# Attention on one core: probabilities turned in 32x32 blocks on VectorE, weighted values on four row tiles of TensorE, and the attention's order taken from a list scheduler

## The chip, the cores and the metric

The kernel runs on one core of one Trainium2 chip. The metric is the device time of one execution in microseconds (us); the times given are medians of three runs. A core has five instruction streams that run side by side and wait for each other through semaphores: TensorE (matmul; PE in the profile, and PEld for its weight loads), VectorE (DVE), ScalarE (ACT), GpSimd (POOL) and SyncE (SP), which here only issues DMA transfers. Each stream runs its instructions in the order in which they stand.

## The reference

The kernel computes one gated block on four batches of 512 tokens with 256 features. Cut to what matters:

```python
xn = layernorm(x)                                     # no affine part
Q, K, V = xn @ Wq + bq, xn @ Wk + bk, xn @ Wv + bv    # 16 query heads, 4 key heads, 128 wide
scores = einsum("blhe,bmhe->bhlm", Q, K) / sqrt(128)
attn = softmax(scores + causal_mask)                  # 512 x 512 per head
ctx = einsum("bhlm,bmhe->blhe", attn, V).reshape(b, l, 2048)
r = xn + gelu(ctx @ Wo + bo)                          # exact GELU
s = (r - mean(r)) * rsqrt(var(r) + 1e-5) * gamma + beta
gate, up = split(xn @ w_gate_up.T)                    # 1024 each
g = silu((silu(gate) * up) @ w_down.T)
out = x + s * g
```

All operands are float32.

## The kernel before

Products of float32 operands are made of three matmuls each: every operand is kept as `hi` (rounded) and `lo` (the exact rest), and `product` (line 93) adds hi*hi, hi*lo and lo*hi into one bank of PSUM. In the profile these three are lines 95, 96 and 97. `split_psum` (line 82) makes the two parts out of a bank: ScalarE writes `hi` (line 86, or 89 with a bias), VectorE writes `lo` (87, or 90).

The first stage computes layer norms and the feed-forward gates of all four batches. The rest, the attention, has 64 steps `(b, g, i)`: batch, key head (with its four query heads) and tile of 128 queries. One batch and key head make a group of four steps; there are 16 groups. For each step:

- `scores` (line 416), four times, for sub-tiles of 32 queries of four heads: a product into bank `ps`, VectorE masks it and takes the row's minimum (449), ScalarE takes exp and the row's sum (460), VectorE the reciprocal (473), GpSimd scales the row (474). The scores are causal: tile `i` and sub-tile `t` see 128 i + 32 (t + 1) keys. For `i = 0` the product is one plain float32 matmul on operands `q0`, `k0` that GpSimd sums from their two parts (`whole`, line 370).
- `transposed_probs` (476), once for each of the `i + 1` blocks `j` of 128 keys: four TensorE transposes into bank `pt` (481), then `split_psum` into `pT`.
- `weighted` (486), once for each block: one product of `v` (128 keys by 128 features, stationary) and `pT` (128 keys by 512 columns: four heads, 128 queries) into bank `pc`. After the last block, `split_psum` makes `ctxT`.
- `projected` (505), once for each of the four heads: a product of 256 columns into the accumulator `py`.

A group thus has 10 blocks `j`. Besides, each group makes the queries of the next group (four products of 512 columns) and its keys, and each batch makes four tiles of values.

PSUM has eight banks: two for `ps`, two for `pt`, one each for `mm` (queries, keys, values), `c` (`pc`), `y0` and `y1` (`py`). All weights stay in SBUF, split once, when they are loaded (lines 111 and 112, on GpSimd in the attention).

The order of the attention's instructions is made in the source by sorting the pieces of a step on hand-set positions (`TUNE`, `ahead`, `chunks`), and the tile framework's own scheduler then orders the streams.

Of the kernel before, what the change touches and what calls it, by code (L numbers as in the profile page):

```python
# [17 lines left out]
P = 128  # L18
EPS = 1e-5
S = 32  # queries of a head in a tile of scores  # L20
MASK = -1e9
HIGHEST = 3.4028235e38
TUNE = {'a0': 0.119, 'a1': 0.3, 's0': 0.673, 's1': 0.335, 't0': 0.293, 't1': 0.231, 'w0': 0.519, 'w1': 0.5, 'o0': -0.076, 'o1': 0.537, 'gelu_at': (0, 1), 'gelu_pos': 0.0, 'fin_g': 1, 'fin_pos': 0.616, 'gelu_behind': 'ctx', 'qd': (1, 2, 1, 0), 'l0': 0.295, 'l1': 0.095, 'l2': 0.234, 'end': {'tab': -1.229, 'T1': 0.136, 'W1': 0.362, 'T0': 0.1, 'W0': 1.019, 'Ob': 0.072, 'Obs': 0.05, 'O1': 0.6, 'O1s': 0, 'O0': 1.0199999999999998, 'key': 'ctx', 'keyb': 'pT', 'G3': 0.1, 'F3': 0.101, 'Gb': 0.5, 'Fb': 0.65, 'vec': True}}
# [3 lines left out]
def kernel(  # L27
    ctx: ExitStack,
    tc: tile.TileContext,
    x: bass.AP,  # [B, L, D]  # L30
    wq: bass.AP,  # [D, H*E]
    bqT: bass.AP,  # [E, H]
    wk: bass.AP,  # [D, KV*E]
    bkT: bass.AP,  # [E, KV]
    wv: bass.AP,  # [D, KV*E]
    bvT: bass.AP,  # [E, KV]
    wo: bass.AP,  # [H*E, D]
    bo: bass.AP,  # [D]
    gamma: bass.AP,  # [D]
    beta: bass.AP,  # [D]  # L40
    wguT: bass.AP,  # [D, 2*INTER]
    wdT: bass.AP,  # [INTER, D]
    out: bass.AP,  # [B, L, D]
):
    """Products of float32 operands run on the tensor engine as products of two
    parts each: hi, rounded to the engine's 12 significant bits, and lo, the exact
    rest. hi*hi + hi*lo + lo*hi, summed in float32, is the float32 product."""
# [6 lines left out]
    G = H // KV  # query heads of a key head: g, g + KV, ...  # L54
    INTER = wdT.shape[0]
    NT = L // P  # token tiles of a batch
    ND = D // P  # chunks of the model dimension
    NI = INTER // P  # chunks of the inner dimension
# [7 lines left out]

    latest = {}

    @contextmanager
    def behind(*keys):  # L70
        """Queues what the block does behind these instructions on their engines."""
# [42 lines left out]
    def load_w(name, views, hi_on=None, lo_on=None):  # L114
# [12 lines left out]
        for k in range(1024 // n):  # L127
            split_sbuf(
                (w[:, 0, ts(k, n)], w[:, 1, ts(k, n)]), st[:, ts(k, n)], hi_on or nc.gpsimd, lo_on or nc.gpsimd
            )  # L130
# [618 lines left out]
```

## Time and profile before

| | us |
|---|---|
| median of 3 runs (680.44 to 681.06) | 680.44 |
| span of the profiled execution | 679.5 |
| TensorE busy | 661.7 (97%) |
| VectorE busy | 447.8 (66%) |
| ScalarE busy | 402.6 (59%) |
| GpSimd busy | 273.4 (40%) |

The profiled execution has its own time, a span of 679.5 us from its first to its last instruction; the runs shown are 0.9 us above it. A row for a group of instructions names line, engine, operation, written and read tiles, shape and count, then the busy time in us, the mean duration of one in ns, and the idle time just before them with what ended it. Durations of matmuls overlap, since matmuls are pipelined: what one costs is seen in the distance from its start to the next start, in the timeline.

### The profile page before, as it was taken

What the parts mean: (1) busy time and instruction counts of PE and PEld (TensorE: products, weight loads), DVE (VectorE), ACT (ScalarE), POOL (GpSimd) and SP (SyncE); (2) the same over time, 40 slices, a digit from 0 to 9 for tenths busy, and PEclk for the clock granted to TensorE, in tenths of its full rate; (3) what the DMA queues carried; (4) which work ended last, traced back from release to release, by engine and by line L of the source; (5) the groups of instructions that cost most, each with busy time, mean ns of one, the idle gap of its engine ahead of it and who ended that gap; (6) DMA issues with size and microseconds to landing.
All of it is one profiled execution on the core that took longest, in us unless ns stands there. A gap on an engine that the chain in (4) does not pass through costs nothing.

```text
span 679.5 us, 12006 instructions
## 1 busy us (share of the span) xinstructions
PE 661.7 (97%) x3996; PEld 581.6 (86%) x3996; DVE 447.8 (66%) x1337; ACT 402.6 (59%) x956; POOL 273.4 (40%) x490
## 2 busy tenths in 40 slices
PE   7979999999999999999999999999999999999995
PEld 6768888889889888888888898889888988888984
DVE  5864434165766766775787666668867766687867
ACT  4434333253765766677676665957666668576772
POOL 5588130720646423222353232216433323354332
PEclk8999999999999999999999999999999999999998
DMA  7753322211310100000022000002210000032000
GB/s 223 246 191 122 127 81 90 77 47 50 92 31 2 36 29 1 1 0 1 20 76 94 1 0 1 2 1 63 63 62 1 1 2 1 1 93 79 1 1 32
DMA packets 25262, 34.73 MB, mean 51 GB/s; under 512 B 2288, under 2 KB 18544, under 8 KB 25200
## 3 DMA queue, kind: packets, MB, share of 16 engines
q1 hardware_dynamic: 25200, 33.97, 15.4%
q8 instruction: 31, 0.51, 0.3%
q14 instruction: 31, 0.25, 0.1%
HBM read 21.38 MB, written 12.58 MB: 50 GB/s over the span
## 4 chain that ended last, share of the span: by engine, by line
PE 89%; DVE 4%; DMA 4%; issue 1%; ACT 1%; POOL 1%; SPq 0%; ACTq 0%; DVEq 0%; POOLq 0%
PE pt L481 10%; PE pc L96 5%; PE pc L95 5%; PE pc L97 5%; PE pq L95 5%; PE py L97 4%; PE ps L97 4%; PE ps L96 4%; PE pq L97 4%; PE pq L96 4%; PE py L95 4%; PE ps L95 4%; PE py L96 4%; PE pg L97 3%; PE pg L96 3%; PE pg L95 3%
## 5 line engine op out<-in xcount | busy, mean ns | idle before, releaser
L474 POOL TENSOR_SCALAR p<-p,total 128x320 f32<-128x320 f32 (+15 forms) x256 | 127.6, 505 | 195.5 <-DVE total L473 174.9
L460 ACT ACTIVATE p<-p,least 128x320 f32<-128x320 f32 (+15 forms) x256 | 133.2, 522 | 59.7 <-DVE least L449 51.0
L449 DVE CUSTOM_DVE_ANT_0 p<-ps,mask 128x320 f32<-128x320 f32 (+15 forms) x256 | 109.8, 435 | 42.6 <-PE ps L97 17.5
L86 ACT CAST pT<-pt 128x512 fp32r<-128x512 f32 x160 | 89.2, 587 | 60.0 <-PE pt L481 59.2
L87 DVE TENSOR_TENSOR pT<-pt,pT 128x512 fp32r<-128x512 f32 x160 | 106.6, 686 | 25.5 <-ACT pT L86 25.0
L481 PE MATMUL pt<-ident,p 128*128 128x128 f32 x640 | 107.2, 273 | 0.5 <-POOL p L474 0.5
L481 PEld LDWEIGHTS pt<-ident,p 128*128 128x128 f32 x640 | 81.1, 142 | 17.5 <-POOL p L474 0.7
L97 PE MATMUL py<-w_o,ctxT 128*128 128x256 f32 x256 | 73.5, 287 | 0.6 <-DVE ctxT L90 0.6
L95 PE MATMUL py<-w_o,ctxT 128*128 128x256 f32 x256 | 72.9, 285 | 0.1
L96 PE MATMUL py<-w_o,ctxT 128*128 128x256 f32 x256 | 72.1, 281 | 0.0
L96 PE MATMUL pc<-pT,v 128*128 128x512 f32 x160 | 69.1, 432 | 0.0
L95 PE MATMUL ps<-kT,qT 128*128 128x288 f32 (+3 forms) x192 | 68.5, 357 | 0.0
L373 POOL TENSOR_TENSOR q<-qT 128x128 f32<-128x128 f32 x64 | 30.4, 474 | 93.7 <-DVE qT L90 55.8
L95 PE MATMUL pc<-pT,v 128*128 128x512 f32 x160 | 64.5, 403 | 0.1
L97 PE MATMUL pc<-pT,v 128*128 128x512 f32 x160 | 63.2, 395 | 0.0
L473 DVE RECIPROCAL total<-total 128x1 f32<-128x1 f32 x256 | 38.4, 158 | 37.2 <-ACT p L460 35.1
L96 PE MATMUL ps<-kT,qT 128*128 128x288 f32 (+3 forms) x192 | 62.2, 324 | 0.0
L97 PE MATMUL ps<-kT,qT 128*128 128x288 f32 (+3 forms) x192 | 61.7, 322 | 0.0
L90 DVE SCALAR_TENSOR_TENSOR qT<-pq,bq_sb,qT 128x512 fp32r<-128x512 f32 x64 | 47.9, 748 | 15.3 <-ACT qT L89 15.3
L89 ACT ACTIVATE qT<-pq,bq_sb 128x512 fp32r<-128x512 f32 x64 | 44.0, 687 | 20.1 <-PE pq L97 19.6
L90 DVE SCALAR_TENSOR_TENSOR ctxT<-pc,bv_sb,ctxT 128x512 fp32r<-128x512 f32 x64 | 47.8, 747 | 11.1 <-ACT ctxT L89 10.5
L95 PE MATMUL pg<-xT,w_gu 128*128 128x512 f32 (+1 forms) x132 | 50.5, 397 | 3.9 <-DVE h L338 2.5
(127 smaller groups left out, 1567.5 us busy)
## 6 DMA issues: line engine op xcount, KB each, us to landing
fin<-fin_dram SPq DMA_DIRECT2D x16, 384.0 KB, 3.2
xT_dram<-xT SPq DMA_DIRECT2D x8, 512.0 KB, 2.6
fin_dram<-gate SPq DMA_DIRECT2D x16, 256.0 KB, 2.0
xT_again<-xT_dram SPq DMA_DIRECT2D x8, 512.0 KB, 3.9
fin_dram<-xn SPq DMA_DIRECT2D x16, 128.0 KB, 2.4
st_q<-in_wq_dram SPq DMA_DIRECT2D x8, 256.0 KB, 3.2
st_o<-in_wo_dram SPq DMA_DIRECT2D x4, 512.0 KB, 3.9
out_dram<-y SPq DMA_DIRECT2D x16, 128.0 KB, 1.7
```

Source lines behind the costliest of these rows:

```text
L86: first = nc.scalar.copy(hi, src)
L87: second = nc.vector.tensor_tensor(lo, src, hi.bitcast(F32), ALU.subtract)
L89: first = nc.scalar.activation(hi, src, AF.Identity, bias=bias)
L90: second = nc.vector.scalar_tensor_tensor(lo, src, bias, hi.bitcast(F32), ALU.add, ALU.subtract)
L95: nc.tensor.matmul(out_ap, lhs[0], rhs[0], start=first, stop=False, **kw)
L96: nc.tensor.matmul(out_ap, lhs[0], rhs[1], start=False, stop=False, **kw)
L97: nc.tensor.matmul(out_ap, lhs[1], rhs[0], start=False, stop=last, **kw)
L449: nc.vector.tensor_tensor_reduce(pr, ps[:, :seen], mask[:, L - seen :], scale=-SCALE, scalar=HIGHEST, op0=ALU.add, op1=ALU.min, accum_out= ...
L460: exp = nc.scalar.activation(pr, pr, AF.Exp, bias=least[:, r : r + 1], scale=-1.0, accum_out=total[:, r : r + 1],)
L473: latest["dve"] = [nc.vector.reciprocal(total[:, r : r + 1], total[:, r : r + 1])]
L474: latest["pool"] = [nc.gpsimd.tensor_scalar(pr, pr, total[:, r : r + 1], 1.0, ALU.mult, ALU.mult)]
L481: nc.tensor.transpose(pt[:, :, t], p[:, t, ts(j, P)], ident)
```

## The change

1. **Weighted values on four row tiles.** The four heads' probabilities of a sub-tile lie on four groups of 32 partitions. Before, full transposes on TensorE brought keys to the partitions. Now VectorE transposes within blocks of 32x32 (`turn`), which leaves the heads on their four groups of 32 partitions and brings 32 keys of each 128 to the partitions of each group. A matmul then contracts over only 32 keys, on 32 rows of the array, and four of them, one a head, go to four row positions and four PSUM banks. The values are laid out to match: written to DRAM when made (`values_out`) and read back four times, once for each group of partitions (`values_beside`).
2. **Two query tiles in a task.** `weighted` handles the pair of tiles `i = 2h, 2h + 1`; blocks `j` seen by both move 256 columns, the last block 128.
3. **Parts.** ScalarE writes `hi` of the turned probabilities from SBUF, GpSimd writes `lo` (on VectorE before). The plain queries `q0` come from ScalarE (from GpSimd before).
4. **Order.** Every instruction of the attention belongs to a task with an engine, a cost, a key and predecessors; class `Order` lists them by key on modelled engines, and pins the outcome as the order of each engine.
5. **Space.** PSUM: four banks for the weighted values, two (`s`) for scores, queries, keys and values, `y0`, `y1`. One tile of probabilities per `i`. Weights of queries and output are split in batch 0, written to DRAM, and read back for each later group.

```diff
+class Order:
+    def keep(self, ins):
+        before = self.last.get(ins.engine)
+        if before is not None:
+            self.tc.add_manual_dep(
+                ins, before.name,
+                mybir.DependencyInfo(mybir.DependencyClass.NoSync, mybir.DependencyReason.DATA),
+                reason="order",
+            )
+        self.last[ins.engine] = ins
...
-        latest["dve"] = [nc.vector.reciprocal(total[:, r : r + 1], total[:, r : r + 1])]
+    def inverse_total(b, g, i):
+        _, total = probs[b, g, i]
+        dve.reciprocal(total, total)
...
-    def transposed_probs(b, g, i, j):
-        pt = psum.tile([P, G, NT, S], F32, tag="t", bufs=2, name=f"pt_{b}_{g}_{i}_{j}")
-        for t in range(NT):
-            nc.tensor.transpose(pt[:, :, t], p[:, t, ts(j, P)], ident)
-        t = pair("pt", 4, f"pT_{b}_{g}_{i}_{j}")
-        latest["pT"] = split_psum(t, pt.rearrange("p r t n -> p (r t n)"))[:1]
+    def turn(b, g, i, j):
+        u = work.tile([P, NT, NT, S], F32, tag="u", bufs=3, name=f"pu_{b}_{g}_{i}_{j}")
+        dve.transpose(u, p_tiles[i][:, :, ts(j, P)].rearrange("p t (c k) -> p c t k", k=S))
+        turned[b, g, i, j] = u.rearrange("p c t q -> p c (t q)")
+    def turned_hi(b, g, i, j):
+        act.copy(part_of(b, g, i, j)[:, 0], turned[b, g, i, j])
+    def turned_lo(b, g, i, j):
+        t = part_of(b, g, i, j)
+        pool.tensor_tensor(t[:, 1], turned.pop((b, g, i, j)), t[:, 0].bitcast(F32), ALU.subtract)
-        product(pc, (v[:, 0], v[:, 1]), (t[:, 0], t[:, 1]), j == 0, j == i)
+    def weighted(b, g, h):
+        for j in range(2 * h + 2):
+            t = pT.pop((b, g, h, j))
+            v = vr[b, g, j // 2]
+            first = 0 if j < 2 * h + 1 else 1
+            for c in range(NT):
+                for a, d in ((0, 0), (0, 1), (1, 0)):
+                    for r in range(G):
+                        pe.matmul(
+                            banks[:, r, h, first * P :],
+                            v[ts(r, S), (j % 2) * NT + c, a],
+                            t[ts(r, S), d, c].rearrange("p i n -> p (i n)"),
+                            start=j == 0 and c == 0 and a == d,
+                            stop=c == NT - 1 and a == 1 and j >= 2 * h,
+                            skip_group_check=True,
+                            tile_position=(r * S, 0),
+                        )
+    def values_beside(b, g, h):
+        vr[b, g, h] = work.tile([P, n, 2, E], F32R, tag="w", bufs=12, name=f"vr_{b}_{g}_{h}")
+        for r in range(G):
+            sp.dma_start(
+                vr[b, g, h][ts(r, S)].rearrange("p c s e -> p c (s e)").bitcast(F32),
+                v_dram[b][g, ts(h, L // 2)].rearrange("(c k) s e -> k c (s e)", k=S),
+            )
+    def load_group(kind, ph):
+        if b == 0:
...
+        else:
+            sp.dma_start(to[ph].bitcast(F32), w_dram[kind, g])
...
+    def columns(n):
+        return max(0.107, 0.00044 * n + 0.007)
...
+                    add("N", "POOL", 0.24 + 0.00083 * seen, key + K["n"], normalized, a, after=[("R", b, g, i)])
...
+                    add("T", "DVE", 0.6, key, turn, a, after=[("N", b, g, i, t) for t in range(NT)], takes="u")
+                    add("H", "ACT", 0.52, key + K["h"], turned_hi, a, after=[("T", *a)] + done, gives=(("u", *a),))
+                    add("L", "POOL", 1.27, key + K["l"], turned_lo, a, after=[("H", *a)], gives=(("u", *a),))
+            fours = (8 * h + 4) * 3 * 0.120 + 12 * 0.112
...
+            add("W", "PE", fours + 0.23, st + K["w"], weighted, (b, g, h), after=deps)
```

Tasks are named by letters that the text below uses: `S` scores, `M` mask, `E` exp, `R` reciprocal, `N` normalize, `T` turn, `H` and `L` the two parts, `W` weighted values, `C` its parts, `Y` projection. `done` for `H` is the `W` task of the group before, since `pT` and the values share twelve slots (`w`) with the weights and `pT` has one slot per block. All instructions recorded through `Order` carry line 47, that of the wrapper, and are told apart by their tiles.

## The prediction

> **What bounds the kernel now.** I read the page first (busy shares, chain, groups), then the busy time of stretches, then TensorE's timeline.
>
> ```profile
> span 679.5 us, 12006 instructions
> PE 661.7 (97%) x3996; PEld 581.6 (86%) x3996; DVE 447.8 (66%) x1337; ACT 402.6 (59%) x956; POOL 273.4 (40%) x490
> ...
> PE 89%; DVE 4%; DMA 4%; issue 1%; ACT 1%; POOL 1%; SPq 0%; ACTq 0%; DVEq 0%; POOLq 0%
> ...
> L87 DVE TENSOR_TENSOR pT<-pt,pT 128x512 fp32r<-128x512 f32 x160 | 106.6, 686 | 25.5 <-ACT pT L86 25.0
> L481 PE MATMUL pt<-ident,p 128*128 128x128 f32 x640 | 107.2, 273 | 0.5 <-POOL p L474 0.5
> ...
> L96 PE MATMUL pc<-pT,v 128*128 128x512 f32 x160 | 69.1, 432 | 0.0
> ```
>
> The chain is 89% TensorE. The stretches place its waits:
>
> ```profile
> 240.00:369.00 129.00, 128.49 (x794) 113.61 (x793) 91.77 (x299) 87.01 (x212) 46.58 (x93) 1.00 0.08 26
> ...
> 660.00:672.00 12.00, 11.43 (x73) 9.87 (x74) 8.64 (x21) 6.36 (x12) 2.54 (x4) 1.00 0.03 12
> 672.00:679.50 7.50, 0.55 (x5) 0.35 (x3) 4.69 (x15) 0.58 (x2) 1.89 (x3) 0.70 0.16 54
> ```
>
> Columns: length, busy us of PE, PEld, DVE, ACT, POOL, then clock and DMA. One batch, 129 us, leaves TensorE 0.5 us idle at full clock: the attention is bound by matmul issue, and only the last 7 us is another engine's. So a matmul removed there is worth its distance to the next start. Timeline (start, duration, both us):
>
> ```profile
> 423.35 0.28 PE L97 MATMUL py<-w_o,ctxT 128*128 128x256 f32 x1
> 423.47 0.28 PE L95 MATMUL py<-w_o,ctxT 128*128 128x256 f32 x1
> 423.59 0.28 PE L96 MATMUL py<-w_o,ctxT 128*128 128x256 f32 x1
> 423.70 0.28 PE L97 MATMUL py<-w_o,ctxT 128*128 128x256 f32 x1
> 423.82 0.60 PE L481 MATMUL pt<-ident,p 128*128 128x128 f32 x4
> 424.18 0.48 PE L96 MATMUL pc<-pT,v 128*128 128x512 f32 x1
> 424.49 0.40 PE L97 MATMUL pc<-pT,v 128*128 128x512 f32 x1
> 424.72 0.40 PE L95 MATMUL pc<-pT,v 128*128 128x512 f32 x1
> ```
>
> A 256-column matmul takes 0.119 us, a 512-column one 0.231. Four transposes take 0.36 and delay the product behind them (0.31 to the next start instead of 0.23): 0.44, so 0.109 each.
>
> **The change, part by part.**
>
> *Transposes leave TensorE*: 640 x 0.109 = -69.8 us.
>
> *Old weighted values leave*: 160 x 3 x 0.231 = -110.9 us.
>
> *New weighted values come.* A group has 48 fours (four row-tiled matmuls, one a head) of 256 columns and 24 of 128; 16 groups have 768 and 384, 4608 matmuls. If a four costs what one full matmul of its width costs, it is 768 x 0.119 + 384 x 0.109 = 133.3 us. The trace shows no row tiling. Upper bound, the four in turn: 4 x 133.3 = 533 us. Lower: no gain below one matmul's streaming, 133.3. I take 133.3: what four heads need is then the old columns (12 x 256 for two query tiles against 2 x 3 x 512), and the planner's cost of a four, 0.120 and 0.112, stands in a list whose other entries the trace confirms: 0.00044 n + 0.007 gives 0.232 for 512 columns (0.231), normalizing 0.24 + 0.00083 x 512 = 0.665 us (0.697 long), hi from SBUF 0.52 (L342's cast, 0.62 long). That is an argument, not a row.
>
> *Entering and leaving row tiling*, 64 times. Between 0 and a full 0.28 us matmul duration (18 us); the nearest row is the 0.085 us a product loses behind a transpose: +5.4 us.
>
> [...]
>
> *VectorE* loses `lo` (160 x 0.686 = 110), gains 160 turns. A turn of 512 columns isn't in the trace: between 0.42 us (VectorE's addition of 256 columns, L522) and 1.37 (two passes of L87); I take one pass, 0.69. It stays near 65%, off the path. *ScalarE*: 160 hi at 0.62 instead of 0.587, 64 short `q0` activations of about 0.39: +30 us, about 66%. Costed at nothing, hidden under TensorE; either engine binds only above 28 us a group, where each needs about 19 to 21.
>
> *GpSimd* gains 160 `lo`; the row is L112's subtraction, 1.31 us median (1.28 to 1.74): +210 us, and loses 64 `q0` sums (-30). A group: 16 normalizations x 0.505 = 8.1, 10 x 1.31 = 13.1, one `k0` 0.5: 21.7 us, against TensorE's new group: queries 5.5, keys and values 2.8, scores about 6, projection 48 x 0.119 = 5.7, weighted 8.3 + 0.3: 28.7 us. So it has 7 us of slack, except in batch 0, where `Order` gives it five slots of weights, each 2 x (0.62 + 1.31) = 3.9 us: three groups x 21.7 + 19.5 = 85 against 3 x 28.7 = 86. Following its stated order there, the weight splits stand ahead of the `lo` of groups 1 and 2, and the first weighted task of each waits some 1 to 2 us: +4 us. Weighted matmuls wait block by block, so a task may start while the last `lo` are made. Steady groups: I allow 0.2 us each, +3.
>
> *The end.* In the last group `hi` of all ten blocks waits for both weighted tasks of the group before. From there TensorE has 7.2 us of scores and projections, then weighted 8.5, projection 5.8: 21.5. GpSimd has three `lo` (3.9), four normalizations (2.6, ready late), a turn and a cast (1.5), four `lo` (5.2), eight normalizations (2.9), three `lo` (3.9): about 20 before the last 2.8 us of weighted values can start, then parts and 5.8 of projection: 28.5. +7 us. Behind it, one more query tile finishes than before, its residual on GpSimd (0.74) instead of VectorE (0.42): +0.7. At the front, scores of the first group run among the gates, as the order shows: 0.
>
> *DMA.* 32 MB of values come back, 24 MB of weights, 16 MB are written: 72 MB on top of 34.7. A group moves 4 MB in 28 us, 143 GB/s; the first slices carried 223 to 246. The path: after a group's last weighted task, 1 MB in four issues of 0.59 us (the `st_q` rows, landing 3.2 us later), some 6.5 us, against 9.4 us of TensorE work before the next needs it. SP issues some 12 transfers a group, 7 us of its time. Costed at 0; each missing us costs 15. Upper end, half speed (10.6 us): +18.
>
> *Order pins* add no instruction; what is late on an engine's head delays what stands behind, as above.
>
> Sum: -69.8 - 110.9 + 133.3 + 5.4 + 4 + 3 + 7 + 0.7 = -27.3 on 679.5: 652.2 us span. The runs lie 0.9 above the profiled span: **653 us**.
>
> **Rivals.** *Slower: row tiles don't overlap as assumed.* Place: the 1152 fours. All other terms together are -160.6 us, so break-even is 0.140 us a four on average (0.116 assumed). Each matmul comes with its own weight load, and in bursts of transposes a load and its matmul take 0.107 us or more; were the four loads serial, a four would cost 0.43: 1152 x 0.43 = 495, total about 1015 us. At 0.2 (half serial): 750. For it: no row shows more than one load and one matmul in 0.107 us. Against: the weights of a four take 32 rows each, and the planner's price. Partial overlap, 0.14 to 0.16: 681 to 704.
>
> *A feeding stall takes the gain.* GpSimd rises from 40 to about 70%, and normalize, turn, hi, lo is a chain of four engines ahead of each weighted task, with one slot a block and two banks for all products but these. At 1 to 2 us a group: 666 to 682. For: L112's slow instances (1.74). Against: 7 us of slack.
>
> *The order hides everything*: stalls 4, 3 and 7 at zero, drains between 0 and 5.4: 634 to 639.
>
> **How the numbers follow.** Main case 0.63 (own range 640 to 666); order hides all 0.06; feeding stall 0.12 (0.09 of it still faster, 0.01 level); partial overlap 0.09 (0.01 faster, 0.01 level); serial 0.10. The range 634 to 692 leaves out serial and half of partial overlap, 0.15 together. A difference of 0.2% is about what a measurement can tell from none. Faster: 0.63 + 0.06 + 0.09 + 0.01 = 0.79; same 0.02; slower 0.02 + 0.07 + 0.10 = 0.19.
>
> **What would show it.** A four at 0.12 between starts of every fourth `banks` matmul; no PE row on `pt`; GpSimd `lo` rows near 1.3 us, its share near 70%; idle ahead of `banks` matmuls below 1 us a group, most in batch 0 and the last group, released by GpSimd `pT`. Fours above 0.14, idle ahead of `banks` put down to DMA `vr`, or turns above 1 us would make it wrong.

## The result and the profile after

| | before | after |
|---|---|---|
| median of the runs compared, us | 680.75 (680.44 to 681.82, 4 runs) | 690.56 (687.05 to 692.98, 4 runs) |
| span of the profiled execution, us | 679.5 | 687.1 |

The changed kernel is slower by 1.4%: ratio 1.014, 95% interval 1.0107 to 1.0172. The prediction was 653.0, faster. The time is inside the range of 634 to 692, but the sign is wrong. The profiled execution of after is the run of 689.51 us, 1.1 us below the median; its span is 687.1. What follows divides up the 7.6 us between the two profiled spans, where the medians lie 9.8 us apart.

The page of after, in the order of the lines shown of before (span, engines, the chain, groups, and the queue that brings code):

```profile
span 687.1 us, 18820 instructions
PE 642.8 (94%) x7484; PEld 572.3 (83%) x7484; DVE 424.8 (62%) x1143; ACT 423.2 (62%) x1027; POOL 442.0 (64%) x585
q8 instruction: 58, 0.95, 0.6%
PE 56%; DVE 9%; issue 4%; POOL 3%; ACT 2%; DMA 0%; POOLq 0%; DVEq 0%; ACTq 0%
...
L47 POOL TENSOR_TENSOR pT<-pu,pT 128x512 fp32r<-128x512 f32 x160 | 203.6, 1299 | 20.9 <-ACT pT L47 20.8
...
L47 PE MATMUL banks<-pT,vr 32*128 32x256 f32 (+1 forms) x4608 | 144.7, 279 | 2.5 <-POOL pT L47 1.5
L47 PE MATMUL py<-w_o,ctxT 128*128 128x256 f32 x768 | 120.3, 291 | 6.4 <-issue 4.2
```

TensorE is busy 19 us less, and it is no longer the whole chain: 56% where it was 89%. No busy share says where the rest is; the stretches do (length, busy us of PE, PEld, DVE, ACT, POOL, then clock, DMA share and GB/s):

```profile
437.27:561.54 124.27, 121.40 (x1665) 110.03 (x1664) 86.66 (x249) 89.31 (x228) 88.18 (x117) 1.00 0.66 180
640.00:656.00 16.00, 14.85 (x247) 13.34 (x243) 8.54 (x30) 9.17 (x27) 12.26 (x18) 1.00 0.01 3
656.00:672.00 16.00, 12.59 (x145) 11.77 (x138) 4.55 (x8) 5.09 (x7) 3.79 (x4) 0.57 0.00 1
672.00:687.10 15.10, 2.43 (x21) 2.23 (x19) 7.58 (x23) 1.60 (x5) 5.49 (x8) 0.72 0.29 87
```

The first row is one batch: 124.3 us instead of 128.9, where the prediction's sum needs about 119 (128.9, less a quarter of the 42.0 us saved on TensorE, plus a quarter of the 3 for steady groups). The last three are the end: the clock falls to 0.57 in the midst of TensorE's last work, and 15 us follow in which TensorE does little; before, the clock was 1.00 up to 672 us and 7.5 us followed.

To compare the two I cut TensorE's time up by the distances between the starts of its matmuls. A gap over 0.1 us in which nothing runs is a *wait* where a semaphore released it and a *stop* where the trace shows nothing that was waited for ("issue"). In stretches of half granted clock, half of the matmul time is counted as *half clock*. What lies before the first and behind the last start stands by itself; the remainder is *matmuls at full clock*.

| us | matmuls at full clock | half clock | waits | stops | before first, after last start | span |
|---|---|---|---|---|---|---|
| before | 660.3 | 1.7 | 8.5 | 0 | 9.0 | 679.5 |
| after | 635.8 | 7.7 | 24.6 | 4.2 | 14.8 | 687.1 |
| difference | -24.5 | +6.0 | +16.1 | +4.2 | +5.8 | +7.6 |
| predicted | -42.0 | 0 | +14.0 | 0 | +0.7 | -27.3 |

So the saving was 17.5 us too large, and 17.4 us of losses were missed. That the waits come near the predicted ones (16.1 against 14.0) is luck: 2.0 us of the growth lie before 90 us and 7.3 between 150 us and the first weighted matmul, where the prediction had none; 3.1 in the groups up to 640 us and 3.7 at the end, 6.8 where it had 14. TensorE's timeline (start, duration, both us; a bracket gives the idle time ahead and who ended it) shows one of each kind: a weighted task at its predicted price, a stop within a product, and the waits of the end with half clock behind them.

```profile
190.92 2.99 PE L47 MATMUL banks<-pT,vr 32*128 32x256 f32 x96
...
297.26 1.07 PE L47 MATMUL py<-w_o,ctxT 128*128 128x256 f32 x7
299.52 0.39 PE L47 MATMUL py<-w_o,ctxT 128*128 128x256 f32 x2 [1.18 <-issue]
...
650.71 5.76 PE L47 MATMUL banks<-pT,vr 32*128 32x256 f32 x188 [0.50 <-POOL pT L47]
657.51 0.39 PE L47 MATMUL banks<-pT,vr 32*128 32x256 f32 x4 [1.04 <-ACT pT L47]
658.85 5.17 PE L47 MATMUL banks<-pT,vr 32*128 32x256 f32 x92 [0.95 <-POOL pT L47]
664.87 0.80 PE L47 MATMUL py<-w_o,ctxT 128*128 128x256 f32 x2 [0.85 <-ACT ctxT L47]
666.23 8.20 PE L47 MATMUL py<-w_o,ctxT 128*128 128x256 f32 x46 [0.57 <-DVE ctxT L47]
```

The 92 matmuls at 658.85 take 5.17 us, the 96 of the same kind at 190.92 take 2.99: half clock. Three stops of this kind stand at 299.5 (1.18 us), 423.6 (1.08) and 547.0 (1.99).

The hand-over from the gates to the attention lost its order. Before, line 459 held the first exponential back until the last gate was through ScalarE: `with behind("gate") if (b, g, i) == (0, 0, 0) else nullcontext():`. The change dropped this guard. ScalarE's timeline after:

```profile
158.84 1.28 ACT L47 ACT_TABLE_LOAD   x1
160.14 0.32 ACT L47 ACTIVATE p<-p,least 128x32 f32<-128x32 f32 x1
...
161.19 1.28 ACT L477 ACT_TABLE_LOAD   x1 [0.64 <-PE banks L213]
162.48 0.60 ACT L477 ACTIVATE h<-banks 128x512 f32<-128x512 f32 x1
163.09 1.28 ACT L47 ACT_TABLE_LOAD   x1
```

Exponential, SiLU, exponential: a table load of 1.28 us ahead of each change of function, nine between 158.8 and 182.2 us where before has one, at 168.25. TensorE pays for it, as its timeline shows:

```profile
163.85 0.50 PE L211 MATMUL banks<-xT,w_gu 128*128 128x512 f32 x1 [1.29 <-DVE h L478]
...
174.80 0.39 PE L211 MATMUL pd<-w_d,hq 128*128 128x256 f32 x1 [1.69 <-ACT gate L493]
```

From 150 us to the first weighted matmul TensorE waits 7.9 us (before: 0.6).

### The profile page after: what moved, and what is told of

Read it like the earlier page. It is cut to its first block, busy times and chain, and to the rows that moved or that the text cites. A ratio compares the mean times of both kernels' runs of the same rounds, so it can differ in the third digit from the quotient of the medians.

```text
span 687.1 us, 18820 instructions
## 1 busy us (share of the span) xinstructions
PE 642.8 (94%) x7484; PEld 572.3 (83%) x7484; DVE 424.8 (62%) x1143; ACT 423.2 (62%) x1027; POOL 442.0 (64%) x585
## 4 chain that ended last, share of the span: by engine, by line
PE 56%; DVE 9%; issue 4%; POOL 3%; ACT 2%; DMA 0%; POOLq 0%; DVEq 0%; ACTq 0%
PE banks L47 18%; PE ps L47 12%; PE pq L47 10%; PE py L47 10%; PE pk L47 3%; DVE p L47 3%; PE pv L47 2%; POOL pT L47 2%; DVE pu L47 2%; DVE ctxT L47 1%; DVE y L47 1%; ACT ctxT L47 1%; POOL p L47 1%; DVE st L47 0%; DMA fin<-fin_dram 0%
## 5 line engine op out<-in xcount | busy, mean ns | idle before, releaser
L47 POOL TENSOR_TENSOR pT<-pu,pT 128x512 fp32r<-128x512 f32 x160 | 203.6, 1299 | 20.9 <-ACT pT L47 20.8
L47 POOL TENSOR_SCALAR p<-p,total 128x256 f32<-128x256 f32 (+15 forms) x256 | 123.6, 501 | 87.9 <-DVE total L47 87.4
L47 ACT ACTIVATE p<-p,least 128x256 f32<-128x256 f32 (+15 forms) x256 | 132.1, 517 | 46.8 <-DVE least L47 42.3
L47 DVE CUSTOM_DVE_ANT_0 p<-ps,mask 128x256 f32<-128x256 f32 (+15 forms) x256 | 108.0, 433 | 72.9 <-PE ps L47 71.5
L47 PEld LDWEIGHTS banks<-pT,vr 32*128 32x128 f32 x4608 | 139.7, 189 | 11.7 <-ACT qT L47 4.3
L47 PE MATMUL banks<-pT,vr 32*128 32x256 f32 (+1 forms) x4608 | 144.7, 279 | 2.5 <-POOL pT L47 1.5
L47 PE MATMUL py<-w_o,ctxT 128*128 128x256 f32 x768 | 120.3, 291 | 6.4 <-issue 4.2
L47 DVE STREAM_TRANSPOSE pu<-p 128x512 f32<-128x512 f32 x160 | 108.8, 696 | 27.6 <-POOL p L47 18.8
L47 PE MATMUL ps<-kT,qT 128*128 128x480 f32 (+11 forms) x576 | 115.8, 328 | 5.4 <-DVE least L47 4.2
L47 PEld LDWEIGHTS py<-w_o,ctxT 128*128 128x128 f32 x768 | 108.7, 194 | 11.6 <-issue 4.5
L47 PEld LDWEIGHTS ps<-kT,qT 128*128 128x128 f32 x576 | 87.0, 188 | 14.8 <-DVE least L47 9.6
L478 DVE TENSOR_TENSOR h<-h,banks 128x512 f32<-128x512 f32 x24 | 16.4, 685 | 56.1 <-ACT h L477 56.0
```

What stands on the lines that cost most here:

```text
L47: made = getattr(self.engine, name)(*args, **kw)
L478: nc.vector.tensor_tensor(h, h, ps[1], ALU.mult)
```

## The experiments

They ask four things: what the row-tiled matmuls cost; whether the hand-over, the feeding chain or the end holds the lost time; what the stops are; and what the half clock costs. A kernel's time is its median, followed by its ratio to the runs of before on the same chip with the 95% interval. The names in brackets are those by which the expectations call a run.

### What the row tiles cost

**Three matmuls of a head together** (e4) instead of four heads in turn:

```diff
-                for a, d in ((0, 0), (0, 1), (1, 0)):
-                    for r in range(G):
+                for r in range(G):
+                    for a, d in ((0, 0), (0, 1), (1, 0)):
```

> The 12 matmuls of a sub-block are the same, but the three of one head stand together, so that neighbours are on the same 32 rows instead of on four different ones. Theory (row tiles run side by side only when neighbours lie on different rows): of each three, the second and third wait for the one ahead, about 0.119 us each, 8 times in 12: some 0.95 us a sub-block instead of 0.36; 384 sub-blocks give +200 to +300 us, and a weighted task of 96 matmuls takes 7.5 to 11 us instead of 2.92. Rival (the engine pairs row tiles in any order): under +20 us.

693.67 us (one run). The first short task's 96 matmuls take 3.01 us (2.99 after). The expected loss isn't there: three in a row on the same 32 rows cost nothing.

**Twelve of a head together** (e8):

```diff
-            for c in range(NT):
-                for a, d in ((0, 0), (0, 1), (1, 0)):
-                    for r in range(G):
+            for r in range(G):
+                for c in range(NT):
+                    for a, d in ((0, 0), (0, 1), (1, 0)):
```

> In each block the 12 matmuls of one head stand together, then the next head's. With three together the order made no difference (a short task took as long as before). Theory (each row group has a queue of its own that holds a few matmuls, so that short runs on one group still overlap with the others): with 12 in a row the queue fills, and a short task takes 5 to 11 us instead of 2.9, the span grows by 80 to 300 us. Rival (order plays no part): 2.9 us, span within 4 us of 690.

1227.01 us (one run). The same first task:

```profile
190.13 11.02 PE L47 MATMUL banks<-pT,vr 32*128 32x256 f32 x96
```

11.02 us instead of 2.99, partly at half clock: the granted clock is half in the last 5.2 us of this task. The whole weighted work is 630 us in distances between starts, half clock included (mean clock of the run 0.735). In the stretches at full clock a matmul of 256 columns takes 0.094 us on average and 0.116 in the median, where the change's order has 0.031 on average and a full matmul takes 0.119: nearly serial. Overlap is thus lost between three and twelve in a row on the same rows, and the order of the change is far from it. That the time rises is what the expectation's theory said; a queue of its own for each group of rows is an assumption of that theory, and no run shows it. What the prediction's rival feared, that matmuls on four different groups of rows run one after the other, no run shows.

**Only head 0's matmuls** (e7; three quarters of the weighted matmuls left out):

```diff
-                    for r in range(G):
+                    for r in range(1):
```

> Leaves out the weighted values of three of the four heads: only the matmuls on the first 32 rows are issued, 1152 instead of 4608. Theory (four row tiles run side by side, one alone is no faster): a matmul of 256 columns takes 0.119 us to the next start, a short task of 24 matmuls 2.7 to 2.9 us as with all 96, and the span changes by under 10 us. Rival (a matmul on 32 rows takes a quarter of the time, by itself): 0.03 us each, a short task takes 0.7 us, and TensorE's weighted work falls by about 105 us.

751.24 us (one run). TensorE's timeline, then a stretch:

```profile
193.79 2.98 PE L47 MATMUL banks<-pT,vr 32*128 32x256 f32 x24
```

```profile
208.67:221.55 12.88, 12.88 (x65) 12.54 (x65) 5.42 (x17) 6.08 (x14) 10.90 (x13) 0.60 0.52 136
```

24 matmuls of one head take 2.98 us, 96 of four heads 2.99: three heads are free, and a four costs what one matmul costs. At 256 and 128 columns, the widths here, that is a factor of 4.0 over four heads in turn (4 x 2.98 / 2.99). The expectation for the span missed: with a quarter of the work the kernel is 60 us longer, since the granted clock falls to half (0.60 on average here) while TensorE is busy for 12.88 of 12.88 us. Half clock, counted as in the table above, is 89 us of its span (7.7 after).

### The hand-over, the feeding and the end

**The guard put back** (e1):

```diff
+        with behind("gate") if (b, g, i, t) == (0, 0, 0, 0) else nullcontext():
-        act.activation(
+            act.activation(
```

> One line of the kernel before is put back: the first exponential of the attention stands behind the last silu of the gates on ScalarE. In the changed kernel ScalarE loads a table 9 times between 158 and 184 us (1.28 us each), because exponentials of the first group stand among the silus, and TensorE waits there 1.29, 0.99, 1.09, 1.69 us for h, hw and gate. Theory (the tables are the hand-over's loss): 17 table loads become 9, these waits go, the first weighted task starts 5 to 8 us earlier than 190.9, and the time falls by about the same, to 682 to 685 in the median against 690.6. Rival (the two banks of s and VectorE's masks bound the hand-over): the exponentials now come in one row behind the gates, scores wait for them, and the time stays within 2 us or grows.

689.02 us, 1.0094 (1.0066 to 1.0122). Table loads fall from 17 to 9, and the waits on ScalarE's `h`, `hw` and `gate` are nearly gone. A new one stands in their place; TensorE's timeline, then VectorE's:

```profile
181.32 5.88 PE L47 MATMUL ps<-kT,qT 128*128 128x256 f32 x21 [3.79 <-DVE least L47]
```

```profile
180.84 0.18 DVE L47 RECIPROCAL total<-total 128x4 f32<-128x4 f32 x1 [1.37 <-ACT p L47]
```

The exponentials now come behind the gates, and in VectorE's pinned order a reciprocal that needs them stands ahead of the masks that TensorE needs. From the last wait that both kernels share (at 90 us) to the first weighted matmul it is 101.3 us instead of 102.0. The cause was right, its price not: 0.7 us come back there, not the 7.9 of waits. Of what was saved, 1.7 us went to half clock behind the new wait.

**The guard, with the scheduler told so** (e11; ScalarE counted as busy for 4 us at the start of its list):

```diff
+    order.task(("silu",), "ACT", 4.0, -100.0, lambda: None)
```

> The guard of e1, and ScalarE counted as taken for its first 4 us in the list, with nothing else moved (e5 also moved four pieces of work out of the gates, and VectorE's order then made TensorE wait 6.24 us for the lo part of values). Theory (the table loads cost what they delay, if VectorE's masks no longer stand behind a reciprocal): no wait of the scores above 1 us between 175 and 192 us, the first weighted task 3 to 5 us earlier than in e1 (192.3), median 684 to 688. Rival (TensorE has nothing else to do until the first exponentials are through): the wait is the same in sum, the median 688 to 692.

691.42 us, 1.0142 (1.0112 to 1.0172). Waits of 2.9 and 2.3 us stand at 182.7 and 191.7: put off, not removed.

**The guard, 8 us, and more of the first group's work in the list** (e5; values 2 and 3, keys 1 and their read-back moved from the front into it):

```diff
-        if t < 2:
-            values(0, t + 2)
-        elif t == 2:
-            keys(0, 1)
...
+    order.task(("silu",), "ACT", 8.0, -100.0, lambda: None)
...
-        if b and g == 0:
-            for t in range(NT):
+        if g == 0:
+            for t in range(NT) if b else range(2, NT):
```

> The guard of the first exponential is put back as in e1, and the list is told of it: ScalarE counts as taken for its first 8 us, and four pieces of work that stood among the gates (two tiles of values, the keys of the second group, the reading back of the first values) become tasks of the list, so that TensorE has them to do while the exponentials catch up. In e1 the guard alone gave under 1 us up to the first weighted task, since VectorE's pinned order put a reciprocal that waits for exponentials ahead of the masks (3.79 us wait of the scores). Theory (the hand-over's loss is an order made for engines that are thought free): 9 table loads, no wait above 1.5 us between 160 and 192 us, first weighted task 5 to 8 us earlier than in e1, the median at 681 to 685. Rival (two banks for scores, queries, keys and values can't feed it): waits of the same sum move elsewhere, the median within 2 us of 689.

704.88 us, 1.0306 (1.0254 to 1.0359): worse. The work moved there lacked cover: a single wait of 6.2 us for `v` on VectorE at 188.7 us, ahead of the `pv` products, and 19.4 us of half clock in all (7.7 after).

**No feeding chain at all** (n1; E, R, N, T, H and L left out in every group; the weighted matmuls take the values as both operands):

```diff
+                    if True:
+                        continue
                     add("E", "ACT",
...
-                            t[ts(r, S), d, c].rearrange("p i n -> p (i n)"),
+                            v[ts(r, S), (j % 2) * NT + c].rearrange("p s e -> p (s e)")[:, first * P :],
```

> Leaves out what lies between the masked scores and the weighted values in every group: exponential, row sum, normalization, turn, hi and lo. The weighted matmuls have the same shapes, rows and number, with the values as their moving operand too. So TensorE keeps all its matmuls and loses nearly all that it waits for. Theory (the sum over TensorE in the prediction was right but for the transposes, and the feeding took the rest): from the distances of starts, 139.5 weighted + 342 scores, queries, keys, values, projection + 153 gates and norms + some 10 at both ends = 645 us of span; with code stops of 4 to 7 us it is 645 to 655. Rival (the matmuls around the row-tiled ones have become dearer in themselves): 665 us or more.

694.48 us (two runs), 1.0169 (1.0105 to 1.0233). GpSimd is busy 17% of the span instead of 64, ScalarE 26 instead of 62, and nothing is gained. The waits of TensorE show why (tiles written, what was waited for, us in all, times, longest):

```profile
PE banks L47 <- issue: 9.9, 5, 3.1
...
PE banks L47 <- DMA vr<-v_dram: 2.3, 3, 1.2
```

What the chain no longer holds up runs into the values' transfers and into stops of up to 3.1 us; half clock rises from 7.7 to 15.2 us, and waits fall only from 24.6 to 20.6. Leaving the feeding out thus gains nothing in time; what it costs by itself this run doesn't show, since other losses take its place. One trace of it remains: the matmuls other than the weighted ones take 489.6 us at full clock instead of 496.0.

**The same in the first group only** (n2):

```diff
+                    if ph == 0:
+                        continue
```

> The same left out in the first group alone. Theory (the hand-over from the gates to the attention, where TensorE stands 8 to 9 us between 158 and 190 us, is lost to feeding): the first weighted task starts 7 to 9 us earlier than 191 to 192 us, and the span falls by 6 to 10 us. Rival (the wait is only put off to the second group): the first weighted task is early, but the span within 3 us of 690.

694.51 us, 1.0159 (1.0106 to 1.0212). From 150 us to the first weighted matmul, now at 169.2 us, TensorE waits 1.4 us instead of 7.9, but the time doesn't shrink: from there to 640 us waits are 6.0 us (3.5 after) and stops 5.8 (4.2). Put off, as its rival said.

**The same in the last group only** (n3):

```diff
+                    if ph == NPH - 1:
+                        continue
```

> The same left out in the last group alone. Theory (late parts of the last group delay the last weighted tasks and bring the half clock): the last two weighted tasks take 8.7 to 9.5 us instead of 15.1, the projection behind them 6 to 7 instead of 9, and the span falls by 9 to 14 us. Rival (the clock falls in any case, and the rest of the end is the same): at most 5 us.

689.38 us, 1.0104 (1.0042 to 1.0166), 2.5 us below after by the two ratios, whose intervals overlap, instead of the expected 9 to 14. TensorE does its part as expected: the last two weighted tasks take 8.65 us without a wait, and from their start to the end it is 33.9 us instead of 37.3. But its profiled execution has a stop of 2.97 us at 549.6 with 6.8 us of half clock behind it.

**Half of the last group's `lo` on VectorE** (e3):

```diff
+                    eng, cost = ("DVE", 0.69) if last_ph and j % 2 else ("POOL", 1.27)
-                    add("L", "POOL", 1.27, key + K["l"], turned_lo, a, after=[("H", *a)], gives=(("u", *a),))
+                    add("L", eng, cost, key + K["l"], turned_lo, a, after=[("H", *a)], gives=(("u", *a),))
```

> In the last group alone the low parts of the odd blocks (5 of 10) are made on VectorE instead of GpSimd. Theory (GpSimd's row of low parts, 649.4 to 660.0 us without a gap, delays the last weighted task, and the waits bring the half clock of 658 to 672): the last two weighted tasks take 9 to 11 us instead of 15.1, less of the projection runs at half clock, and the span falls by 5 to 9 us. Rival (the clock falls in any case when the work thins out, or the turns are as late as before): at most 2 us.

691.8 us, 1.014 (1.0118 to 1.0163). From the start of the last two weighted tasks to the end it takes 37.6 us (37.3 after): the delay moved. The normalizations on GpSimd now wait 3.5 us for VectorE (2.0 after), and the last two turns start 7.0 us behind the start of these tasks instead of 6.3. GpSimd's `lo` alone isn't what makes the end late.

**Two of the last four read-backs of the epilogue in tiles of their own** (e2), so that they don't wait for the other two:

```diff
+        tag = "xT" if b == B - 1 and t < 2 else "gate"
-        fin[b, t] = work.tile([P, 3, D], F32, tag="gate", bufs=2, name=f"fin_{b}_{t}")
+        fin[b, t] = work.tile([P, 3, D], F32, tag=tag, bufs=2, name=f"fin_{b}_{t}")
```

> The last two of the four fin loads of the last batch get buffers of their own (the two of xT, free by then) instead of waiting for the first two to be used. Theory (the end of the kernel is a chain of late loads): the residuals of the last two tiles, which ran at 679.6 and 680.9 us behind a wait of 3.15 us for DMA, run at about 677.2 and 677.9; the span falls by 2.5 to 3.5 us. Rival (something else ends last): under 1 us.

692.11 us, 1.0154 (1.0131 to 1.0177). The part behind the last matmul's start shrinks from 13.0 to 10.8 us, nearly as expected; in its profiled execution a stop of 2.3 us at 646.9 and half clock behind it take that back.

**This, the Gelu table loaded ahead, and the parts of query tiles 2 and 3 before the last task** (e9):

```diff
+                add("GT", "ACT", 1.3, key, gelu_table, (), after=[("H", b, g, 1, j) for j in range(2)])
...
+            if last_ph and h == 0:
+                deps += [("Cl", b, g, i) for i in (2, 3)]
```

> Three repairs of the end that keep all work: own buffers for the last two fin loads (as e2, where the time from the last weighted task to the end fell by 2.3 us), the Gelu table loaded ahead (1.28 us between the last ctxT and the first y), and the parts of the context of query tiles 2 and 3 made before the last weighted task instead of behind it (ScalarE waited 6.08 us for the banks). Theory: from the start of the last two weighted tasks to the end 32 to 34 us instead of 37.3, the median at 686 to 688. Rival (the parts ahead of the last task cost what they save): 35 us, the median at 689.

694.64 us, 1.0168 (1.0121 to 1.0214). Behind the last start 9.9 us instead of 13.0, but TensorE now waits 3.7 us for those parts, a new wait for the one removed, and half clock is 16.4 us (7.7 after).

### The stops

At 299.5 TensorE waits for nothing that it shares with an engine. What precedes it on SP's DMA queue:

```profile
288.87 0.62 SPq L47 DMA_DIRECT2D w_q<-w_dram_q  x1
289.65 2.16 SPq L47 DMA_DIRECT2D vr<-v_dram  x4
```

That is 2 MB; the DMA engines' share from 290 to 295 us is 1.05. On the instruction queue come blocks of 16 KB, 58 where before has 31. In both kernels that is one for 129 of TensorE's matmuls (7484 / 58 and 3996 / 31), so I take them for TensorE's code. By the distance that other blocks keep to their matmuls, the block for the place of the stop was due to start at about 292.6, an estimate; it starts at 296.39, 3.8 us late, lands at 297.86, and TensorE goes on at 299.52. Ahead of each of the three stops stands such a block, and TensorE goes on 2.6 to 3.1 us after its start. The theory: code comes late behind the values and weights that are read back.

**Half of what is read back** (e6; the values' and the weights' low parts left out, the high ones used twice):

```diff
-            sp.dma_start(to[ph].bitcast(F32), w_dram[kind, g])
+            sp.dma_start(to[ph][:, 0].bitcast(F32), w_dram[kind, g][:, 0])
```

> Leaves out half of the data that is read back: of the values and, from the second batch on, of the weights only the hi parts are loaded, and the matmuls read hi where they read lo. All instructions on the engines stay. Theory (TensorE's code comes in blocks of 16 KB by DMA, some come late behind the transfers of values and weights, and TensorE stops with nothing to wait for): the three stops of 1.1 to 2.3 us ahead of py in each run (4.2 us in all in the changed kernel's profile, 6.7 in another) shrink to under 1 us in all, and the time falls by 3 to 7 us. Rival (the stops belong to the code itself, not to the transfers): they stay at the same three places, and the time within 2 us.

689.18 us, 1.010 (1.0068 to 1.0131). The three stops shrink from 4.2 to 2.0 us in all.

**An eighth of what is read back** (e10; the rest of the values and weights left out, the same columns used again):

```diff
-            sp.dma_start(to[ph].bitcast(F32), w_dram[kind, g])
+            sp.dma_start(to[ph][:, 0, :256].bitcast(F32), w_dram[kind, g][:, 0, :256])
...
-                v_dram[b][g, ts(h, L // 2)].rearrange("(c k) s e -> k c (s e)", k=S),
+                v_dram[b][g, ds(h * (L // 2), S)].rearrange("k s e -> k (s e)"),
```

> Leaves out nearly all data that is read back: an eighth of the values and, from the second batch on, of the weights is loaded (the matmuls read these same columns again and again). All instructions on the engines stay. Half the data gave stops of 0.72, 0.48, 0.84 us (2.0 in all) where the changed kernel has 1.18, 1.08, 1.99 (4.2). Theory (code blocks wait behind these transfers): no stop without a cause above 0.3 us, less than 2 us of half clock in the middle of the kernel, and the median 4 to 8 us below the changed kernel's 690.6. Rival (the stops are the code's own): 2 us of stops remain, the median within 3 us.

684.7 us (8 runs), 1.0044 (1.0025 to 1.0063). No stop is left, and half clock falls to 5.1 us. The matmuls at full clock take the same 635.9 us as after. Against 1.014 that is (1.014 - 1.0044) x 682 = 6.5 us: this is the price of the transfers that the prediction put at 0. In the profiled execution the stops are 4.2 us less than after and half clock 2.6 less, all of that at the end. The code blocks bear the theory out, for TensorE's order is the same in both kernels: the blocks ahead of the three stops start here when TensorE has begun 2398, 4061 and 5707 of its matmuls, after when it has begun 2502, 4160 and 5825, 99 to 118 matmuls later. Not every block that is so late brings a stop: those at 250.72 and 613.10 us are 102 and 111 matmuls late without one.

**One transfer of a batch moved** (e12; the 1 MB of `w_q` behind a weighted task):

```diff
-                done = [("Qp", *divmod(ph - 2, KV), r) for r in range(G)]
+                done = [("Qp", *divmod(ph - 2, KV), r) for r in range(G)] + ([("W", *divmod(ph - 3, KV), 1)] if b and g == 2 else [])
```

> One transfer in each batch from the second on, the weights of its third group's queries (1 MB), is issued behind the second weighted task of the last group of the batch before instead of 1 us before the values of its first group. TensorE's order stays as it is. In the changed kernel the code block that TensorE stops for begins to move at 296.39 us, 3.8 us after TensorE came to the place where blocks are asked for elsewhere, behind these 2 MB. Theory (the block waits behind that transfer): the stops near 300, 424 and 547 us shrink to under 0.5 us each, the median falls by 3 to 6 us. Rival (the values alone, or other transfers, hold it up as long): stops above 1 us, the median within 2 us.

691.64 us, 1.0143 (1.0108 to 1.0178). Of the three stops the first is left, 1.0 us: its code block comes as late as after (2503 matmuls begun), the other two come earlier (4133 and 5749). So this transfer brings two of the three; the time is the same, and its profiled execution has half clock at 175 and 188 us instead.

### The clock

In the record of after the clock falls to half from 658.17 to 671.83 us, 13.65 us or four times the 3.41 of its shortest stretch at half clock (at 9.64 us), behind waits of 0.50, 1.04 and 0.95 us in the 8 us before.

**26 matmuls that compute nothing, in the waits of the last two tasks** (e14):

```diff
+        end = (b, g) == (B - 1, KV - 1)
+        if end:
+            busy(4 if h else 8)
...
+                    if end and h == 0 and (j, c, d) == (0, 0, 1):
+                        busy(7)
```

> Adds 26 matmuls of 256 columns (3.1 us at full clock) on resident weights into an unused bank of PSUM, at the places where TensorE waits in the last two weighted tasks and ahead of the last projection (0.50, 1.04, 0.95, 0.85 us in the changed kernel). Nothing else changes. Theory (the waits bring the half clock, 13.65 us of it from 658 on): the clock stays full there or falls for at most 3.4 us, the last projection of 48 matmuls takes 6 us instead of 9, and from the start of the last weighted tasks to the end it is 32 to 34 us instead of 37.3. Rival (the clock falls with the matmuls on 32 rows, or in any case at the end): 38 to 41 us, since the added matmuls come on top.

687.98 us, 1.0101 (1.0086 to 1.0117). The stretch that had a clock of 0.57, then TensorE's last matmuls:

```profile
656.00:672.00 16.00, 15.14 (x278) 14.28 (x271) 4.97 (x8) 5.99 (x10) 7.12 (x9) 1.00 0.01 3
```

```profile
666.80 5.86 PE L47 MATMUL py<-w_o,ctxT 128*128 128x256 f32 x46 [0.86 <-DVE ctxT L47]
```

Full clock, 5.86 us instead of 8.20 for the same 46 matmuls, and 33.8 us instead of 37.3 from the start of the last tasks to the end. The waits of the end, at most 1.04 us each, cost more through the clock (5.8 us of half clock from 640 us on) than as waits (4.4).

### What beats both kernels

**The guard with 4 us, `w_q` moved, own tiles for the epilogue and the Gelu table ahead** (e13):

> e11 and e12 together with own buffers for the last two fin loads and the Gelu table loaded ahead (in e9 the time behind the last matmul fell from 13.0 to 9.9 us). Theory (the repairs add up): 3 from the end, 3 to 5 from the hand-over, 3 to 6 from the stops: 677 to 682, level with the kernel before. Rival (what is taken away ahead of TensorE comes back as another wait or as half clock): 685 or more.

686.15 us, 1.0064 (1.0042 to 1.0087): better than any of these alone, slower than before.

**This, the 26 matmuls, and the low parts of `w_d` on VectorE instead of GpSimd** (e15):

```diff
-    wd = [load_w(f"d{s}", [wd_v[:, ts(s, 4)]]) for s in range(2)]
+    wd = [load_w(f"d{s}", [wd_v[:, ts(s, 4)]], None, nc.vector) for s in range(2)]
```

> e13 with the matmuls of e14, and the lo parts of the weights w_d on VectorE instead of GpSimd (TensorE waits for them 0.9 to 3.2 us near 30 us, with half clock behind in most runs). Theory: 2 to 4 us less than e13's 686.2 from the end, 1 to 3 from the front: 680 to 683, level with the kernel before (682). Rival: 685 or more.

676.36 us (675.59 to 684.64, 7 runs) against 681.27 of before: 0.9926 (0.9912 to 0.994). This one is faster than both kernels. The profiled execution is the longest of the seven (684.64; the other six lie between 675.6 and 677.7). It still has a stop of 2.1 us at 645.3, so its trace doesn't show how the 9.4 us from the version above divide up. The matmuls in the waits alone are worth 2.7 us (1.014 to 1.0101, intervals that overlap by little); the rest wasn't separated.

## Why the prediction was wrong, point by point

The direction was wrong because the saving on TensorE was priced too high (42.0 us, measured 24.5) and because terms put at nothing, or left out, came to 15.3 us: stops 4.2, half clock 6.0, and 5.1 more behind the last matmul's start. The step that it doubted most, four row tiles at the price of one, held. By term:

- **New weighted values, 133.3, and mode switches, 5.4: right.** Together 138.7; measured 139.8 us at full clock. One against four heads (2.98 and 2.99 us) shows why. The rivals of partial and of serial overlap fall for this order of the matmuls. The 5.4 for the switches had only a far row behind it (0.085 us lost behind a transpose), and no run here measures a switch by itself or shows that TensorE drains there, as the word "drains" in the prediction's last rival has it: the two terms together came within 1.1 us.
- **Transposes and old weighted values, -69.8 - 110.9 = -180.7: 6.6 too much.** Over the whole trace the distances to the next start sum to 54.7 us for `pt` and 119.4 for `pc`, 174.1. The one run of four transposes that I priced was no fair sample: "Four transposes take 0.36 and delay the product behind them" counts 0.109 each, the sum gives 54.7 / 640 = 0.085. The delay of the product behind them lies in `pc`, which holds 8.5 us more than the 110.9 priced, while `pt` holds 15.1 less than 69.8.
- **The other matmuls: no term.** They lengthened by 9.8 us (-24.5 in all, less 139.8 - 174.1): scores 110.8 to 115.0, projections 94.3 to 97.8, queries 90.8 to 92.7, the rest level. Not from the transfers (635.9 us in all with an eighth of the read-back). Some 6.4 us go with the feeding: without any, the same matmuls take 489.6 us instead of 496.0, scores 109.4 and queries 91.5, about as before; the total of 631.9 hides it, since the weighted matmuls of that run, with other operands, take 142.5. Part of it are waits too short for the table: from 150 us on, where another engine's release stands right before a matmul's start and no gap of 0.1 us shows, the distances exceed the planner's price of the matmul ahead by 4.5 us in sum, 1.2 before; 3.6 of it is behind VectorE's `least`, the scores' wait for a free bank. What lengthens the projections by 3.5 us (97.5 without feeding) isn't settled.
- **The front, "as the order shows: 0": wrong.** The order showed the exponentials between the SiLUs, and I read it as more overlap without pricing the change of tables. Nine loads of 1.28 us and 7.9 us of waits (0.6 before) followed. But with the guard back only 0.7 us of it came back up to the first weighted matmul: the first group's own chain is then late. Where between 0.7 us and the 7.3 by which the waits grew the cost of the lost guard lies isn't settled.
- **Steady groups and batch 0, +3 and +4:** from the first weighted task to 640 us waits grew by 3.1 us (0.4 to 3.5), less than the 7 allowed. `lo` took 1.30 us (1.31 predicted), a turn 0.70 (0.69), and GpSimd's share is 64%. The rival of a feeding stall (16 to 32 us) falls: with the 6.4 us above it would be 9.5. The group of 28.7 us, with which the prediction compared GpSimd, doesn't agree with its own sum, by which a group takes (128.9 - 10.5) / 4 = 29.6; it counts the scores at about 6 us, where before has 110.8 / 16 = 6.9. After, a group takes 31.1, so GpSimd had more slack than the 7 us, not less.
- **The end, +7 and +0.7: half of it.** From 640 us waits grew by 3.7, half clock by about 6, and what lies behind the last start by 5.8: 15.5 us. The 7 stood for waits alone. The other two terms, the clock behind short waits and the epilogue's transfers and table load, are missing. Moving work of one engine gave nothing, leaving out the last group's feeding 2.5 us, filling the waits 2.7 us of the whole time.
- **DMA, "costed at 0": wrong by some 6 us,** and not by the path that I checked. The values arrive in time (no wait of TensorE for `vr` above 0.1 us after); code does not. The upper end of 18 us for slower transfers covered its size.
- **The clock: no term.** The 6.0 us more of half clock in the profiled span all lie from 658.2 to 671.8 us, behind the short waits of the end. Behind the three stops this execution has none; in other runs half clock follows such stops (6.8 us behind the stop of 2.97 us in the run without the last group's feeding).

Sum: 6.6 (transposes) + 9.8 (others) + 1.1 (row tiles) + 2.1 (waits, 16.1 against 14) + 4.2 (stops) + 6.0 (clock) + 5.1 (behind the last start) = 34.9, which is 687.1 - 652.2, the distance between the spans. That the time lies inside the range is luck: its upper part, up to 692, stood there for a feeding stall and for row tiles that overlap in part, and neither occurred; their size happened to be that of the terms that were missing.

## What to carry to other kernels

Price what a removed operation saves by the sum of all its distances in the trace, not by one clean spot (0.085 against 0.109 us a transpose), and expect its neighbours to take part of it back (9.8 us here). When a change raises the number of instructions and moves data beside them, ask when the instructions themselves arrive (3.8 us late here, for one stop of 1.18 us); and when TensorE stops being busy without a break, price the clock and not only the wait (5.8 us of half clock behind 4.4 us of waits at the end). A wait at the junction of two stages is only worth removing with the next wait behind it in view: four of the runs here removed one and met another.

## What the runs showed of the hardware that was not expected

- Four row tiles of 32 rows cost what one does (2.99 and 2.98 us for 96 and 24 matmuls of 256 and 128 columns). Three in a row on the same 32 rows are still free (3.01), twelve are nearly serial (11.02, of which 5.2 at half clock; 0.094 us for a matmul of 256 columns at full clock, 0.031 in the change's order).
- The granted clock falls to half behind single stops or waits of 1.5 to 3.8 us (with the guard put back a wait of 3.79 us, 1.7 us of half clock behind it; in the run with own tiles for the epilogue a stop of 2.34 us at 646.9, half clock from 649.35; without any feeding a stop of 1.52 us at 354.1, half clock from 354.60) and behind several shorter ones (in after three that add up to 2.5 us), though not behind each such stop: after the 1.99 us at 547.0 the clock stayed full. In the trace of after it is half for 3.41 us at 9.64 and for 13.65, four times that, from 658.17.
- A TensorE that is busy all the time with matmuls of one 32-row tile among others got a mean clock of 0.60 over 12.88 us; the whole kernel took 751.2 us instead of 690.6, with 89 us of half clock.
- A block of TensorE's code came 3.8 us late behind 2 MB of data and stopped it within a product for 1.2 us; stops reached 3.1 us in the run without feeding. With an eighth of the data the same block starts 104 matmuls earlier, and there is no stop.
